# Head products in smaller pieces, value sums on TensorE for half of the heads stage, and half of the routing scatters behind the next root

## The chip, the core and the metric

The kernel runs on one core of a Trainium2 chip. The core has five engines that work side by side, each through its own queue in order: TensorE (PE in the profile, with PEld for its weight loads), VectorE (DVE), ScalarE (ACT), GpSimd (POOL) and SyncE (SP), which issues transfers here. The metric is the device time of one execution in microseconds (us), the median of several runs. Lower is better.

## The reference

The program is a decoder of two layers, all in fp32, on x of 4 sequences with 256 tokens of 256 features. Every step is `x = x + block(layernorm(x))`. Layer 0 has an attention with a compressed key and value, a cross attention over a context, and a block that routes one token in eight through attention and MLP. Layer 1 has three blocks, and two of them are what this case is about.

The first is an attention over the 16 heads *of one token*, with no product between tokens:

```python
qkv = x @ w_qkv.T + b_qkv                      # (b, n, 3, H=16, d=16)
attn = einsum('bnhd,bngd->bnhg', q, k) / sqrt(c)
attn = softmax(attn, axis=-1)
out  = einsum('bnhg,bngd->bnhd', attn, v)
out  = out.transpose(0, 2, 1, 3).reshape(b, n, c) @ w_out.T + b_out
```

Per token that is a 16x16 table of weights, and each is a sum over 16 products. Then follows a causal cross attention over the context with 16 heads, and last a mixture of 28 experts (width 176): a softmax over 28 gate values, the best six of them made to sum to one, and `y += w * (silu(x @ wg) * (x @ wu)) @ wd` for these six.

## The kernel before

**Layout and order.** The tokens lie on the 128 partitions: each sequence is two tiles of 128 tokens. The program is written as Python generators, which are advanced in turn by `_side_by_side` (L60) with weights, so that instructions of two stages come to lie beside each other. A scheduler then settles the order in each engine's queue from the dependencies. `_stay_behind` (L78) adds a dependency that only fixes the order of two instructions on one queue; no semaphore comes of it. Buffers come from pools; a tile with `bufs=1` can be written again only when its last reader is done.

**Heads stage** (`_head_attention`, L1422). `half(g)` does sequences 0 and 1 (g = 0), then 2 and 3 (g = 1), each in four steps j of 128 rows. `project` (L1475) computes q, k and v on TensorE, which ACT copies into `qkv`. `products` (L1501) lets GpSimd multiply every q by every k: four instructions of 128x1024 in each step, into two tiles `qk` (L1518 for g = 0, L1526 for g = 1). `weights` (L1535) sums them: for g = 0 on TensorE by 16 products with the identity for each half c of the heads, into the PSUM tile `as` (L1545); for g = 1 by DVE reduces (L1562). Then come maximum, subtraction and the exponential on ACT. `combine` (L1569) sums the weights on DVE (L1571), takes the reciprocal (L1573), scales the weights (L1574), multiplies by v into `pv` (128x2048, L1580) and reduces it into `O` (L1587), for each half c. At the end `O` is turned by TensorE (L1604), projected, and added to x (L1619). `products(j+1)` is written ahead of `combine(j)`. g = 0 stands beside the routed block of layer 0 (`_routed_block`: mask L1176, rope steps L1243 on DVE and L1250, L1253 on GpSimd, mpr L1345, maT L1361, and the addition L1310), and the layer-0 cross attention (L596); g = 1 beside the first half of the cross attention.

**Cross attention** (`_cross_attention`, L1628). Eight units for each sequence b. A unit computes scores `xsc` on TensorE, their maximum `cnm` on DVE (L1711, L1712), the exponential `xpr` on ACT (L1717), turns it in TensorE (`x_tp`) and copies it from PSUM to `xpT`: three copies of four on DVE (L1733), one on ACT (L1731). Then `xav`, the projection `xpo`, the addition to x (L1773), and `then(b)`, which starts the routing of that sequence while the units of the next go on. `xqT` (L1821) is the query of a pair of sequences.

**Routing** (`_route`, L698). For sequence b: POOL fills parts of `R` (L704, L706); `layernorm` takes mean and variance on DVE (`ln_ve`, L167), the inverse root by a `pow` on GpSimd (`ln_rs`, L154; the "root" below), and writes R on DVE (L172). TensorE turns it (`g_tp`, L714), computes gate values `pl` (L721), DVE copies them (`lg`, L723) and finds the best six; TensorE ranks the tokens of each expert (`rank`, L761, L762); DVE gives the target `rows` (L770) and the weights (L780). Then twelve indirect transfers by GpSimd, two tiles by six experts, scatter the rows of R into `lists` in memory (L786).

**Experts.** `_Blocks` (L879) works on blocks of 128 rows of `lists`: load `xb` (L917), turn (`tpx`, L923), `pgu` (L933), silu and product (`eh`, L939), turn (L944), the weight of each row (`wjunk`, L953), `py` (L964), `ys` (L968), and an adding scatter into `acc` (L969). There are 62 blocks; the first nine are loaded from GpSimd's queue, the others from SP's. The gate and up weights (`wgu_e`) are loaded after the heads stage, the down weights (`wdn_e`, L678) after the cross attention, both by SP. The nine early loads, the routing of sequence 3 and the first blocks stand beside one another.

Of the kernel before, what the change touches and what calls it, by code (L numbers as in the profile page):

```python
# [10 lines left out]
F32 = mybir.dt.float32  # L11
# [3 lines left out]
ALU = mybir.AluOpType  # L15
# [4 lines left out]
P = 128  # L20
# [99 lines left out]
def kernel(ctx: ExitStack, tc: tile.TileContext, w: dict, out: bass.AP):  # L120
    nc = tc.nc
# [28 lines left out]
    nc.gpsimd.tensor_tensor(root, root, neghalf, ALU.pow)  # L150

    def rsqrt(src, n, tag):
        r = sm.tile([P, n], F32, tag=tag, name=tag)
        nc.gpsimd.tensor_tensor(r, src, neghalf[:, :n], ALU.pow)  # L154
        return r
# [349 lines left out]
    for _ in range(4):  # L505
# [17 lines left out]
        turned32=cst[:, K_TURN:], blank=blank, psum=psum, sm=sm, cst=cst, ident=ident, identb=identb, maskb=maskb, tri=tri, ones=ones,  # L523
        ones_row=ones_row, layernorm=layernorm, ln_stats=ln_stats, ln_apply=ln_apply, rsqrt=rsqrt, transposed=transposed, ctxT=ctxT, neghalf=neghalf,
    )
# [111 lines left out]
    nc.sync.dma_start(wgt, w["e_gate"].rearrange("(k p) n -> p k n", p=P))  # L637
    route = dict(env, rt=rt, rt1=rt1, wgt=wgt, seen=seen, lists=lists)
    xatt = ExitStack()
# [37 lines left out]
    for g in range(0, E, 7):  # L677
# [3 lines left out]
        )  # L681
    blocks = _Blocks(ctx, nc, tc, dict(route, wgu=wgu, wdn=wdn, acc=acc))
    early = blocks.early(*route["early"])
    last = _route(nc, tc, x, B - 1, route)
    for _ in range(2):
        next(last)
    next(early)
    for _ in last:
# [6 lines left out]
def _route(nc, tc, x, b, env):  # L695
# [9 lines left out]
    for i in range(2):  # L705
        nc.gpsimd.iota(  # L706
            R[:, i, C : C + 1].bitcast(I32), [[0, 1]], base=(2 * b + i) * P, channel_multiplier=1
        )
    env["layernorm"](x[2 * b : 2 * b + 2], [R[:, i, :C] for i in range(2)])
    yield  # L710
    tp = psum.tile([P, 2, 2, P], F32, tag="tp", name="g_tp")
# [57 lines left out]
    rows = rt.tile([P, 2, TOPK], I32, tag="rows", name="rows")  # L769
    nc.vector.tensor_scalar(rows, top[:, :, :TOPK], -1.0, None, ALU.add)  # L770

# [8 lines left out]
    nc.vector.tensor_tensor(R[:, :, C + 1 : C + 1 + E], ex, wide(zt), ALU.mult)  # L780

    for n in range(TOPK):
        if b < B - 1 and n:
            yield
        for i in range(2):
            put = nc.gpsimd.indirect_dma_start(  # L786
                out=lists,
                out_offset=bass.IndirectOffsetOnAxis(ap=rows[:, i, n : n + 1], axis=0),
                in_=R[:, i, :],
                in_offset=None,  # L790
            )
            tc.declare_no_dep(put.ins, group="lists", reason="all rows of all of these differ")
            tc.add_to_no_dep_group("lists", put.ins)

# [84 lines left out]
class _Blocks:  # L879
# [5 lines left out]
    def __init__(self, ctx, nc, tc, env):  # L885
        self.nc, self.psum, self.cst, self.ident = (nc, env["psum"], env["cst"], env["ident"])
        self.wgu, self.wdn, self.lists, self.acc = (env[n] for n in ("wgu", "wdn", "lists", "acc"))
        self.ek = ctx.enter_context(tc.tile_pool(name="ek", bufs=2))
        self.eb = ctx.enter_context(tc.tile_pool(name="eb", bufs=EARLY + 2))
        self.puts = 0  # L890

# [22 lines left out]

    def load(self, row, queue):
        xb = self.eb.tile([P, ROW], F32, tag="xb", name="xb")
        queue.dma_start(xb, self.lists[bass.ds(row, P), :])  # L917
        return xb
# [30 lines left out]
    def down(self, hT, e, xb, e_col, accs):  # L949
        nc = self.nc  # L950
        wsel = self.ek.tile([P, 1], F32, tag="wsel", name="wsel")
        junk = self.ek.tile([P, E], F32, tag="wjunk", name="wjunk")
        nc.vector.scalar_tensor_tensor(  # L953
            junk,
            self.cst[:, K_IOTA : K_IOTA + E],
            e_col,
            xb[:, C + 1 : C + 1 + E],
            ALU.is_equal,
            ALU.mult,
            accum_out=wsel,  # L960
        )
        py = self.psum.tile([P, C], F32, tag="o", name="py")
        for k in range(2):
            nc.tensor.matmul(  # L964
                py, hT[:, k, :], self.wdn[:, bass.ds(e * (2 * C) + k * C, C)], start=(k == 0), stop=(k == 1)
            )
        y = self.ek.tile([P, C], F32, tag="ys", name="ys", bufs=NACC + 2)
        nc.scalar.activation(y, py, AF.Copy, scale=wsel)  # L968
        nc.gpsimd.indirect_dma_start(  # L969
            out=accs[self.puts % len(accs)],  # L970
            out_offset=bass.IndirectOffsetOnAxis(ap=xb[:, C : C + 1].bitcast(I32), axis=0),
            in_=y,
            in_offset=None,
            compute_op=ALU.add,
        )
        self.puts += 1

    def early(self, words, rows, e_all):
        at = self.values(rows, mybir.EngineType.Pool, TRASH, 0, EARLY)
        xbs = [self.load(r, self.nc.gpsimd) for r in at]  # L980
        yield
# [439 lines left out]
def _head_attention(nc, tc, x, w, env):  # L1421
# [6 lines left out]
    H = D = 16  # L1428
    Q = S // H

    a1 = env["stack"].enter_context(tc.tile_pool(name="ha1", bufs=1))
# [21 lines left out]
    def half(g):  # L1453
# [46 lines left out]
        def products(j):  # L1500
# [4 lines left out]
            for c in range(2):  # L1505
# [5 lines left out]
                else:  # L1511
                    q3 = qkv[:, 0:C].rearrange("p (h d) -> p h d", d=D)
                    k3 = qkv[:, C : 2 * C].rearrange("p (g d) -> p g d", d=D)
                    pr = a2.tile([P, 8, H, D], F32, tag="qk", name="qk")
                for i in range(2):
                    if g == 0:
                        dd = slice(8 * i, 8 * i + 8)
                        nc.gpsimd.tensor_tensor(  # L1518
                            pr[:, dd],
                            q3[:, dd, hh].unsqueeze(3).to_broadcast([P, 8, 8, H]),  # L1520
                            k3[:, dd].unsqueeze(2).to_broadcast([P, 8, 8, H]),
                            ALU.mult,
                        )
                    else:
                        h0 = 8 * c + 4 * i
                        nc.gpsimd.tensor_tensor(  # L1526
                            pr[:, 4 * i : 4 * i + 4],
                            q3[:, h0 : h0 + 4].unsqueeze(2).to_broadcast([P, 4, H, D]),
                            k3.unsqueeze(1).to_broadcast([P, 4, H, D]),
                            ALU.mult,  # L1530
                        )
# [37 lines left out]
        def combine(j, qkv, s):  # L1569
            ss = sm.tile([P, H], F32, tag="ass", name="ass")  # L1570
            nc.vector.tensor_reduce(ss, s, AX.X, ALU.add)  # L1571
            rs = sm.tile([P, H], F32, tag="ars", name="ars")
            nc.vector.reciprocal(rs, ss)  # L1573
            nc.vector.tensor_tensor(s, s, rs.unsqueeze(2).to_broadcast([P, H, H]), ALU.mult)  # L1574
            yield
            v3 = qkv[:, 2 * C :].rearrange("p (d g) -> p d g", g=H)
            for c in range(2):
                hh = slice(8 * c, 8 * c + 8)
                pv = a2.tile([P, 8, D, H], F32, tag="pv", name="pv", bufs=1)
                nc.vector.tensor_tensor(  # L1580
# [46 lines left out]
def _cross_attention(nc, tc, x, w, env):  # L1627
# [93 lines left out]

    def turned(pr, sp):
        pTs = []
        for j in range(2):
# [4 lines left out]
            pT = c3.tile([P, 3 * P], F32, tag=f"xpT{sp}{j}", name=f"xpT{sp}{j}", bufs=2)  # L1729
            if sp and j:  # L1730
                nc.scalar.copy(pT, tp.rearrange("p n q -> p (n q)"))  # L1731
# [52 lines left out]
    def after(f, b, g, e, sp, pr, ss):  # L1784
# [3 lines left out]
        if sp == 0:  # L1788
            state["pTs"] = turned(pr, sp)
            return  # L1790

        pTs = [one for two in zip(state["pTs"], turned(pr, sp)) for one in two]

# [184 lines left out]
```

## Time and profile before

| what | value |
|---|---|
| median of three runs | 864.11 us (860.93 to 864.4) |
| the profiled execution | 864.99 us |
| its span, first to last instruction | 863.3 us |
| mean granted TensorE clock | 0.887 of full |
| busy, PE / PEld / DVE / ACT / POOL | 693.8 / 456.4 / 531.1 / 295.9 / 323.3 us |
| L1518 and L1526, products on GpSimd | 16 of 2372 ns and 16 of 2371 ns mean |
| L1580, pv on DVE | 16 of 2576 ns mean, 2271 shortest, 4074 longest |
| L1587, reduce on DVE | 16 of 2271 ns mean |
| L1574, scaling of weights on DVE | 8 of 843 ns mean |
| L1545, sums on TensorE (128 products, two records each) | 256 records, 35.7 us |
| L1733 and L1731, copies of xpT on DVE and on ACT | 548 and 482 ns mean |
| L786, scatters on GpSimd | 48, 46.7 us |

How to read it: the profile shows one execution, 1.7 us shorter in its span than in its own time. "Busy" is the time in which an engine executes. A record is "start, length, engine, line, operation, output <- inputs"; in brackets stands how long the engine had been idle ahead of it and which instruction or transfer released it. PEclk is the TensorE clock that was granted, as a share of full speed. The chain of waits is followed back from the last instruction to what released each one.

The heads stage with g = 0 lies at about 300 to 430 us, with g = 1 at 430 to 550, the second half of the cross attention with the routing of sequences 1 and 2 at 565 to 645, the routing of sequence 3 and the first blocks at 645 to 699, and the other blocks from there to 850.

### The profile page before, as it was taken

The page shows a single profiled execution, that of the slowest core. Times are in us where ns is not written, and L with a number is a line of the kernel's source. Part 1 is how long each engine was busy: PE and PEld are TensorE (multiplying, and loading weights), DVE is VectorE, ACT ScalarE, POOL GpSimd, SP SyncE. Part 2 cuts the span into 40 slices and gives each one's busy share as a digit, 9 for nine tenths or more (in the row PEclk, how much of TensorE's full clock was granted, in tenths as well). Part 3 has the DMA queues.
Part 4 walks back from the last instruction along what each step waited for, and adds up shares of the span by engine and source line. Part 5 has one row for each costly group of instructions (what it writes and reads, how often), then busy time and mean ns, then how long its engine had stood idle before and what let it go on. Part 6 is the DMA issues. An engine that isn't in the chain of part 4 may idle for free. (4 is left out here: it accounts for less than half of the span.)

```text
span 863.3 us, 12247 instructions
## 1 busy us (share of the span) xinstructions
PE 693.8 (80%) x3902; PEld 456.4 (53%) x3902; DVE 531.1 (62%) x1322; ACT 295.9 (34%) x974; POOL 323.3 (37%) x277
## 2 busy tenths in 40 slices
PE   8988998598988878869659556978573989889991
PEld 4546556355555566466325234556442667657770
DVE  4677666986563798985549997757352423363332
ACT  2255444342441401221045224355231334324440
POOL 3332212214220365520145430052352675556663
PEclk9999999789999789978789957998685899999995
DMA  8999999400405200231400000680138686776656
GB/s 296 307 332 325 325 327 326 179 1 0 175 27 204 84 2 1 80 116 49 153 13 1 0 1 1 223 329 29 55 102 189 171 149 107 143 190 103 111 69 167
DMA packets 84739, 117.93 MB, mean 137 GB/s; under 512 B 5822, under 2 KB 71871, under 8 KB 84162
## 3 DMA queue, kind: packets, MB, share of 16 engines
q1 hardware_dynamic: 71346, 99.00, 35.4%
q0 software_dynamic: 11664, 16.54, 11.1%
q10 hardware_dynamic: 1664, 1.57, 0.6%
q8 instruction: 35, 0.57, 0.3%
q14 instruction: 30, 0.25, 0.1%
HBM read 59.66 MB, written 55.33 MB: 133 GB/s over the span
## 5 line engine op out<-in xcount | busy, mean ns | idle before, releaser
L969 POOL DMA_INDIRECT acc<-ys,xb x62 | 98.2, 1583 | 60.8 <-ACT Tx L925 50.3
L933 PE MATMUL pgu<-wgu_e,Tx 128*128 x248 | 91.4, 492 | 4.3 <-ACT Tx L925 3.7
L416 POOL TENSOR_TENSOR pr<-pr,rs 128x512 f32<-128x512 f32 x32 | 42.4, 1325 | 131.5 <-DVE rs L414 73.8
L406 ACT ACTIVATE pr<-sc,nb 128x256 f32<-128x256 f32 x128 | 59.0, 475 | 49.4 <-DVE nb L401 49.3
L786 POOL DMA_INDIRECT lists<-R,rows x48 | 46.7, 973 | 67.7 <-DVE rows L770 29.6
L1717 ACT ACTIVATE xpr<-xsc,cnm 128x256 f32<-128x256 f32 (+1 forms) x128 | 52.2, 422 | 53.9 <-DVE cnm L1712 47.3
L964 PE MATMUL py<-wdn_e,Th 88*128 x248 | 64.3, 384 | 3.7 <-DVE Th L946 3.7
L964 PEld LDWEIGHTS py<-wdn_e,Th 88*128 88x128 f32 x248 | 46.8, 192 | 20.5 <-DVE Th L946 5.6
L933 PEld LDWEIGHTS pgu<-wgu_e,Tx 128*128 128x128 f32 x248 | 44.1, 198 | 21.2 <-issue 3.2
L1526 POOL TENSOR_TENSOR qk<-qkv 128x1024 f32<-128x1024 f32 x16 | 37.4, 2371 | 38.5 <-ACT qkv L1497 26.4
L939 DVE TENSOR_TENSOR eh<-pgu,sg 128x176 f32<-128x176 f32 x62 | 21.1, 340 | 49.8 <-ACT sg L937 49.8
L105 PE MATMUL av<-pT,ckt 128*64 128x256 f32 x256 | 39.4, 404 | 14.8 <-DVE pT L432 9.9
L1545 PE MATMUL as<-qk,cst 128*128 128x128 f32 x256 | 35.7, 305 | 10.4 <-POOL qk L1518 10.4
L968 ACT ACTIVATE ys<-py,wsel 128x256 f32<-128x256 f32 x62 | 29.4, 474 | 41.5 <-PE py L964 38.1
L937 ACT ACTIVATE sg<-pgu 128x176 f32<-128x176 f32 x62 | 19.7, 318 | 69.4 <-PE pgu L933 69.4
L1518 POOL TENSOR_TENSOR qk<-qkv 128x1024 f32<-128x1024 f32 x16 | 37.5, 2372 | 13.8 <-ACT qkv L1490 7.1
L397 DVE TENSOR_REDUCE nm<-sc 128x4 f32<-128x1024 f32 x32 | 38.9, 1217 | 5.5 <-PE sc L105 5.2
L953 DVE SCALAR_TENSOR_TENSOR wjunk<-cst,e_all,xb 128x28 f32<-128x28 f32 x62 | 15.4, 248 | 42.5 <-ACT ys L968 37.7
L1545 PEld LDWEIGHTS as<-qk,cst 128*128 128x128 f32 x256 | 34.3, 219 | 13.2 <-POOL qk L1518 11.5
L1580 DVE TENSOR_TENSOR pv<-s,qkv 128x2048 f32<-128x2048 f32 x16 | 41.2, 2576 | 0.1
L108 PE MATMUL tp<-cst,pr 128*128 128x128 f32 x256 | 38.5, 293 | 2.4 <-DVE pT L432 1.5
L105 PE MATMUL sc<-ckv,qk 64*128 64x256 f32 x256 | 39.5, 410 | 0.8 <-ACT qk L383 0.8
(374 smaller groups left out, 1556.5 us busy)
## 6 DMA issues: line engine op xcount, KB each, us to landing
lists<-blank SPq DMA_DIRECT2D x9, 3600.0 KB, 28.5
wgu_e<-in_e_gu_dram SPq DMA_DIRECT2D x4, 2464.0 KB, 16.1
xb<-lists SPq DMA_DIRECT2D x53, 144.0 KB, 2.6
acc<-blank SPq DMA_DIRECT2D x5, 1152.0 KB, 11.2
wdn_e<-in_e_dn_dram SPq DMA_DIRECT2D x4, 1232.0 KB
wq<-in_m_wq_dram SPq DMA_DIRECT2D x4, 1024.0 KB, 6.7
mwo<-in_m_wo_dram SPq DMA_DIRECT2D x2, 2048.0 KB, 8.2
part<-acc SPq DMA_DIRECT2D x16, 256.0 KB, 4.4
```

The costliest lines, as they stand in the source:

```text
L105: self._next(self.engine.matmul(*args, **kw))
L108: self._next(self.engine.transpose(*args, **kw))
L397: nc.vector.tensor_reduce(nm, sc, AX.X, ALU.max, negate=True)
L406: nc.scalar.activation(pr[:, e, qt, :], sc[:, e, qt, :], AF.Exp, bias=nb[:, e, qt : qt + 1], accum_out=ss[:, e, qt : qt + 1],)
L416: nc.gpsimd.tensor_tensor(pr[:, 1], pr[:, 1], rs[:, 1].unsqueeze(2).to_broadcast([P, 2, S]), ALU.mult)
L786: put = nc.gpsimd.indirect_dma_start(out=lists, out_offset=bass.IndirectOffsetOnAxis(ap=rows[:, i, n : n + 1], axis=0), in_=R[:, i, :], in ...
L933: nc.tensor.matmul(pg, xT[:, k, :], self.wgu[:, bass.ds(e * (4 * M) + k * 2 * M, 2 * M)], start=(k == 0), stop=(k == 1))
L964: nc.tensor.matmul(py, hT[:, k, :], self.wdn[:, bass.ds(e * (2 * C) + k * C, C)], start=(k == 0), stop=(k == 1))
L969: nc.gpsimd.indirect_dma_start(out=accs[self.puts % len(accs)], out_offset=bass.IndirectOffsetOnAxis(ap=xb[:, C : C + 1].bitcast(I32), axi ...
L1545: nc.tensor.matmul(ps[:, c, :P], ident, prs[c][:, n].rearrange("p h g -> p (h g)"), start=(n == 0), stop=(n == D - 1),)
L1580: nc.vector.tensor_tensor(pv, s[:, hh].unsqueeze(2).to_broadcast([P, 8, D, H]), v3.unsqueeze(1).to_broadcast([P, 8, D, H]), ALU.mult,)
L1717: nc.scalar.activation(pr[:, j, cols], sc[:, j, cols], AF.Exp, bias=nm[:, i, j : j + 1], accum_out=ss[:, i, h : h + 1])
```

## The change

1. **Pieces.** The products of q and k on GpSimd are issued as four instructions of 512 elements for each tile, not two of 1024 (both g).
2. **Value sums on TensorE**, for g = 1. The weights are not scaled by the reciprocal. `pv` has the layout (g, h, d), so that both inputs are read in steps of 16 elements (64 bytes) along one dimension; sixteen products with the identity for each half c sum it over g into the PSUM tile `ao`, and one DVE operation for each j multiplies by the reciprocal into `O`. `pv` gets two buffers (both g).
3. **Scatters.** For b = 0 and 1 the last six of the twelve scatters are put off (`puts`) and issued, in the queue's order, behind the root of sequence b + 1. The nine early loads are ordered behind the root of sequence 3, and the first `wjunk` behind `rows` of sequence 3.
4. **Copies.** For b = 0 and 1, three of four `xpT` copies go to ACT and one to DVE.

GpSimd's queue from the routing of sequence 0 on is then: six scatters of sequence 0, root of 1, six scatters of 0, memset and iota of R for 2, six scatters of 1, root of 2, six of 1, memset and iota of R for 3, twelve of 2, root of 3, nine loads, twelve of 3. Before it was: twelve of 0, memset and iota for 2, root of 1, twelve of 1, memset and iota for 3, root of 2, twelve of 2, two loads, root of 3, seven loads, twelve of 3. TensorE's order around sequence 3 stays. In the second half of the heads stage the sums `ao` stand between the cross units on TensorE, two of them ahead of each `pqkv` but the first two. In the first half, the last two `pv` now stand ahead of the routed block's second `mpr` and of both `maT`, where one stood ahead of that `mpr` and the other between the two `maT` before.

The core of the diff:

```diff
     def rsqrt(src, n, tag):
         r = sm.tile([P, n], F32, tag=tag, name=tag)
-        nc.gpsimd.tensor_tensor(r, src, neghalf[:, :n], ALU.pow)
+        roots.append(nc.gpsimd.tensor_tensor(r, src, neghalf[:, :n], ALU.pow))
         return r
...
     env["layernorm"](x[2 * b : 2 * b + 2], [R[:, i, :C] for i in range(2)])
+
+    root = env["roots"][-1]
+    for put in env["puts"]:
+        _stay_behind(tc, put(), root)
+    env["puts"] = []
+    env["root"] = root
     yield
...
     for n in range(TOPK):
         if b < B - 1 and n:
             yield
         for i in range(2):
...
+            if b < B - 2 and n >= TOPK // 2:
+                env["puts"].append(functools.partial(put, n, i))
+            else:
+                put(n, i)
...
-    def load(self, row, queue):
+    def load(self, row, queue, behind=None):
         xb = self.eb.tile([P, ROW], F32, tag="xb", name="xb")
-        queue.dma_start(xb, self.lists[bass.ds(row, P), :])
+        done = queue.dma_start(xb, self.lists[bass.ds(row, P), :])
+        if behind is not None:
+            _stay_behind(self.tc, done, behind)
         return xb
...
+        if not self.puts:
+            _stay_behind(self.tc, done, self.route["placed"])
...
-                for i in range(2):
+
+                for i in range(4):
                     if g == 0:
-                        dd = slice(8 * i, 8 * i + 8)
+                        dd = slice(4 * i, 4 * i + 4)
...
                     else:
-                        h0 = 8 * c + 4 * i
+                        h0 = 8 * c + 2 * i
...
+            if g == 1:
+
+                v3 = qkv[:, 2 * C :].rearrange("p (d g) -> p g d", g=H)
+                ps = psum.tile([P, 2, 8, D], F32, tag="o", name="ao")
+                for c in range(2):
+                    hh = slice(8 * c, 8 * c + 8)
+                    pv = a2.tile([P, H, 8, D], F32, tag="pv", name="pv", bufs=PV)
+                    nc.vector.tensor_tensor(
+                        pv,
+                        s[:, hh].rearrange("p h g -> p g h").unsqueeze(3).to_broadcast([P, H, 8, D]),
+                        v3.unsqueeze(2).to_broadcast([P, H, 8, D]),
+                        ALU.mult,
+                    )
+                    yield
+                    for n in range(H):
+                        nc.tensor.matmul(
+                            ps[:, c].rearrange("p h d -> p (h d)"),
+                            ident,
+                            pv[:, n].rearrange("p h d -> p (h d)"),
+                            start=(n == 0),
+                            stop=(n == H - 1),
+                        )
+                    yield
+                nc.vector.tensor_tensor(
+                    O[:, :, j, :],
+                    ps.rearrange("p c h d -> p (c h) d"),
+                    rs.unsqueeze(2).to_broadcast([P, H, D]),
+                    ALU.mult,
+                )
+                return
             nc.vector.tensor_tensor(s, s, rs.unsqueeze(2).to_broadcast([P, H, H]), ALU.mult)
...
-                pv = a2.tile([P, 8, D, H], F32, tag="pv", name="pv", bufs=1)
+                pv = a2.tile([P, 8, D, H], F32, tag="pv", name="pv", bufs=PV)
...
-            if sp and j:
+
+            if (sp and j) if b >= 2 else (sp or j):
                 nc.scalar.copy(pT, tp.rearrange("p n q -> p (n q)"))
```

## The prediction

> **What bounds the kernel now.** I read the windows by stage first, then the chain of waits, then the timelines of the engines at its waits. The windows (core time, then busy time and instructions of PE, PEld, DVE, ACT, POOL, the granted clock, DMA) part the stages:
>
> ```profile
> 320.00:430.00 110.00, 86.37 (x501) 60.32 (x500) 82.05 (x125) 19.19 (x55) 36.96 (x29) 0.86 0.22 73
> 430.00:550.00 120.00, 81.79 (x501) 47.46 (x499) 96.75 (x122) 44.99 (x163) 39.15 (x18) 0.82 0.04 11
> 565.00:660.00 95.00, 63.82 (x484) 45.24 (x482) 48.18 (x163) 33.08 (x140) 42.12 (x53) 0.79 0.39 124
> ```
>
> From 430 to 550 (heads of sequences 2 and 3 beside cross attention) DVE leads with 97 of 120 us, and in finer windows it is busy 20.00 of the 20 us from 480. From 565 to 660 (cross attention and routing) no engine is two thirds busy: waits set the time. The chain of waits there runs through GpSimd's scatters:
>
> ```profile
> 609.51 2.43 DMA lists<-R,rows
> 612.04 2.45 DMA lists<-R,rows
> 614.90 0.70 POOL ln_rs L154
> 616.18 0.66 PE g_tp L714 x2
> ...
> 643.38 9.32 DMA lists<-R,rows
> ```
>
> and TensorE's timeline shows what they cost (start, length, instruction, in brackets the idle time before it and its releaser):
>
> ```profile
> 584.06 0.66 PE L714 MATMUL g_tp<-cst,R 128*128 128x128 f32 x2 [5.58 <-DVE R L172]
> ...
> 616.18 0.66 PE L714 MATMUL g_tp<-cst,R 128*128 128x128 f32 x2 [8.48 <-DVE R L172]
> ...
> 656.01 1.09 PE L714 MATMUL g_tp<-cst,R 128*128 128x128 f32 x4 [12.89 <-DVE R L172]
> ...
> 663.34 0.69 PE L923 MATMUL tpx<-cst,xb 128*128 128x128 f32 x2 [3.13 <-DVE lg L723]
> ```
>
> R waits for the root on GpSimd, and the root for its queue. After 699 the expert blocks follow one another, paced by TensorE (pgu and py), to the end: I take that tail to shift rigidly.
>
> **Scatters behind the root.** The root of sequence 1 could run when ln_ve exists; GpSimd was elsewhere:
>
> ```profile
> 576.44 0.41 DVE L167 TENSOR_SCALAR ln_ve<-ln_mv 128x2 f32<-128x2 f32 x1
> ```
> ```profile
> 579.72 0.96 POOL L786 DMA_INDIRECT lists<-R,rows  x1 [0.30 <-issue]
> 582.51 0.11 POOL L704 MEMSET R<- 128x6 f32 x1 [1.83 <-issue]
> ...
> 582.75 0.72 POOL L154 TENSOR_TENSOR ln_rs<-ln_ve,neghalf 128x2 f32<-128x2 f32 x1
> ```
>
> A scatter takes 0.96 + 0.30 between two = 1.27 us; twelve occupy GpSimd from 565.52 to 580.68. With six deferred it is free at 573.1, before ln_ve at 576.9. Root 0.72, R 0.41 and a hand-over of 0.15 to 0.5 put g_tp at about 578.4, where TensorE arrives at 578.5: 5.58 becomes 0.3, gain **5.3**. For sequence 2, ln_ve is there at 607.9 and six scatters from 598.02 end at 605.6. Root, R and hand-over give 609.3 against TensorE free at 607.7: 8.48 becomes 1.6, gain **6.9**.
>
> The deferred six, 7.6 us, and the memset, which waits 1.6 to 1.8 for the last of them to be read, now lie behind the root. For sequence 1 this ends at 577.7 + 7.6 + 2 = 587; the next rows come at 592.5 (598.0 less 5.3), so they fit with 5 us left. For sequence 2 it ends near 612.5 on the shortened clock against rows near 614: 1.5 us left. If that is eaten, the last scatters land later, and the early loads with them: I take **+0.5**, from 0 to +2. Nobody reads the deferred rows before those loads.
>
> At sequence 3 the root leaves the loads (654.67, behind two of them) for 645.2, ahead of nine. That does not start the experts: the first tpx needs xb, which needs the 9.32 us landing of the last scatter (beside the wdn_e weights, issued from 643.15) and 8.8 of its own load. The loads start where they did. What goes is lg waiting on DVE behind wjunk: xb landed at 662.07 and tpx began at 663.34, so **1.2**. The rank at 668.82 stays behind pgu on TensorE.
>
> After each gap TensorE is slow: the same sixteen xav take 1.51 us at 585.84 and 0.86 at 594.09; six x_tp 1.54 against 0.87; eight xsc 1.36 against 0.92. One gap costs 1.8 us in these rows. The Trainium skill (TensorE: Matmul & The Clock Gate, "Why this matters for your kernels") says that idle gaps over about 3 us drop the clock. By that rule, both gaps being under 3 afterwards, both penalties go in full, 1.8 and about 3. The granted clock rows are less kind: 0.73 in 620 to 640 with TensorE busy 18.45 of 20 us. I take **3**, between 0 and 5.
>
> Sum: −5.3 − 6.9 − 1.2 − 3 + 0.5 = **−15.9**, from −9 to −19.
>
> **Sums on TensorE, and copies to ACT (second half).** DVE loses 8 reduces of L1587 at 2.27 (18.2 us), four L1574 (0.42 clean, up to 2.44: say 4), and 16 copies at 0.55 (8.8). It gains four O operations reading PSUM, 0.42 each as L1619. Net −29 us of 97. ACT gains 16 x 0.48 = 7.7 on 45 of 120: hidden. The eight pv now read s and v in 64-byte steps, as no DVE row here does. Below: 2.28, the clean pv row; above: twice that, +18 on DVE. VectorE: DVE Perf Modes ("Mode 1× (REGULAR) — the baseline") holds that plain fp32 makes no assumption on strides; I take 2.28.
>
> TensorE gains 128 products of fp32 128x128. The row for the same shape is
>
> ```profile
> L1545 PE MATMUL as<-qk,cst 128*128 128x128 f32 x256 | 35.7, 305 | 10.4 <-POOL qk L1518 10.4
> ```
>
> with two records to a product; on the timeline 32 to 36 records pass in 4.2 us, so 0.25 us a product, 32 us in all (36 by busy time). Here the skill speaks for a far better deal: the clock page's "Back-to-back issue gap" gives about 81 ns for N = 128, hence 10 us. The row decides, since it has this type and shape; by the rule TensorE would stay far from full, by the row it fills up: 81.8 + 32 = 114 of 120 us, less what a warmer clock returns (0.82 now). So the bound passes from DVE to TensorE. One sum of 16 products (4.2 us) also stands where a 2.27 us reduce stood in the chain pv, O. And pqkv of the next step stands behind two such sums on TensorE, 8.4 us, with the qk of GpSimd waiting for it; the xsc units stand behind them too, and their cnm on DVE. Against that, DVE waits such as 7.61 us of TensorE on xpT at 499.26 vanish. Walking the new order by these durations, O of the last step comes at 522 to 525 instead of 530.5, but about two cross units are left over that were done before; xqT of the second half, which ends the stage, comes at 556 to 560 instead of 560. I take **−2**, from +6 to −8.
>
> **Products in pieces of 512 (both halves).** 32 instructions become 64. A clean piece should take about half of 2.03 plus a start: L416, also 512 wide, has a mean of 1.325, clean L1250 1.27, so 1.05 to 1.3, or 0.1 to 0.5 for each of 32 extra, 3 to 9 us of GpSimd, which idles two thirds of these stages; on the path only where qk is waited for, some 2 us. What it buys: DVE operations with two SBUF inputs stand while a product runs:
>
> ```profile
> 479.79 4.07 DVE L1580 TENSOR_TENSOR pv<-s,qkv 128x2048 f32<-128x2048 f32 x1
> ```
>
> Clean, this pv is 2.28; the excess of 1.8 is nearly one whole product. I sum such excesses to 17 us on DVE in the first half (L1580, L1574, L1176, L1243, L596, L1310). If a stall lasts to the end of the running piece, half, 8 us, goes; about 5 of it lies on the routed chain. Against it: two pv buffers let the scheduler put both last pv ahead of the routed block's mpr and maT, up to two more operations of 2.28, about +1.8 there once other waits overlap, and GpSimd's extra +1 in the rope steps (L1250, L1253). Net **−2**, from +3 to −6.
>
> **Total.** −15.9 − 2 − 2 = −19.9 on the profiled execution's 864.99 (span 863.3 and 1.7 around it): **845**. The median of the runs is 0.9 lower, within my rounding.
>
> **Rivals.**
> 1. *The routing waits are replaced.* For: only 1.5 us of cover at sequence 2, and the landing beside wdn_e (9.32 against 2.45) may grow. Then the first wait's 5.3 and 1.2 are kept, 6.9 and the clock are halved, +2 is paid: −9.5; heads nothing: **855**.
> 2. *The heads give all their room.* DVE's full stretch was the bound and TensorE's clock warms to 1.00, as in 460 to 480 with 17.97 busy: −8 and −5 beside −17: **835**.
> 3. *TensorE as the new bound; slower.* Place: 449 to 550. At the slow clock of that stage (0.15 a record) the 128 products cost 38 us, as much as all idle there (120 − 81.8 = 38.2), and idle cannot be packed: each of eight sums then adds its 4.2 in full, 34 us, less the 8 of shortening I granted and the 16 of routing: +10, **875**. It decides from the point where the heads stage loses more than 20 us, that is when over 60% of the new products fall outside the idle time. Against it: DVE's own work drops by 29 us, so TensorE's waits on DVE shrink.
> 4. *Order eats all.* The stage loses 12 to 18 (or pv pays its +18 for the strides), cancelling routing: **863**.
>
> **Numbers.** A measurement of this kernel tells about 0.5%, 4.3 us, from no change. Forecast 0.51 (838 to 852), rival 1 0.18, rival 2 0.11, rival 4 0.09, rival 3 0.11. Faster: 0.51 + 0.18 + 0.11 = 0.80; same 0.09; slower 0.11. The range 829 to 863 leaves out rival 3 and a little at each end.
>
> **What would show it.** Right: g_tp waits under 2 us at sequences 1 and 2, the root of sequence 3 before the first load, tpx still waiting for xb; ao at about 4.2 us for a sum, TensorE above 90% from 449 to 540; pv near 2.28 with excesses under 1.2; the block tail as long as before. Wrong: pv near 4.5 in the second half; xqT of the second half later than 565; a memset or scatter on GpSimd that waits longer than 2 us ahead of the root; lists landing later than 9.3 after its last scatter.

## The result, and the profile after

The changed kernel takes 876.12 us (875.0 to 877.25, four runs) against 864.01 for the kernel before (four runs beside it): a ratio of 1.0148, 95% interval 1.0121 to 1.0175. It is slower; 845 had been forecast. Its profiled execution took 875.67 us, its span is 873.7, or 10.4 more than before. Code below the first part of the change has other line numbers now (pv of the second half is L1603, the sums are L1611, the scatters L792, the root L157).

The first view is the windows again, cut this time at events that both kernels have: from the first products of the second half of the heads to the last `o_tp`, from there to the last `xqT`, and on to the issue of the wdn_e loads, which follows the end of the cross attention. Of before:

```profile
437.90:535.40 97.50, 59.56 (x381) 34.61 (x380) 84.93 (x90) 37.59 (x135) 37.45 (x16) 0.79 0.00 1
535.40:560.90 25.50, 23.89 (x156) 15.17 (x154) 18.80 (x65) 10.05 (x41) 1.71 (x2) 1.00 0.50 186
560.90:643.20 82.30, 64.71 (x514) 45.58 (x514) 48.18 (x162) 35.49 (x149) 36.04 (x43) 0.83 0.34 127
```

The same three of the changed kernel:

```profile
442.50:553.20 110.70, 85.00 (x623) 64.23 (x621) 67.45 (x68) 37.94 (x133) 40.49 (x32) 0.85 0.00 1
553.20:585.30 32.10, 28.65 (x175) 18.82 (x171) 19.03 (x70) 14.84 (x57) 4.88 (x6) 0.89 0.75 281
585.30:653.20 67.90, 62.26 (x510) 43.81 (x510) 46.57 (x154) 36.26 (x151) 33.58 (x41) 0.90 0.25 93
```

The routing stretch fell by 14.3 us, near the sum that was worked out. The two stretches of the heads grew by 13.2 and 6.6: TensorE (the first busy number) gained 25 us, VectorE (the third) lost 17, and the stage became longer though VectorE is now idle for two fifths of it. The first half of the heads (first products to the products of the second half) went from 139.5 to 144.6. So −0.6 ahead of it, +5.2 + 19.8 − 14.3, and +0.3 behind: 10.4.

TensorE's waits in the routing, the answer to the four lines shown of before:

```profile
603.65 0.44 PE L723 MATMUL g_tp<-cst,R 128*128 128x128 f32 x2 [0.47 <-DVE R L175]
...
626.24 0.41 PE L723 MATMUL g_tp<-cst,R 128*128 128x128 f32 x2 [1.60 <-DVE R L175]
...
656.49 0.67 PE L723 MATMUL g_tp<-cst,R 128*128 128x128 f32 x4 [3.27 <-DVE R L175]
...
668.17 0.66 PE L941 MATMUL tpx<-cst,xb 128*128 128x128 f32 x2 [8.41 <-DMA xb<-lists]
```

0.47 and 1.60 us stand where 5.58 and 8.48 stood. The wait of sequence 3 went from R to xb, as expected, and the end does not hang on it: the first `py` waits for the down weights.

```profile
693.02 3.75 PE L984 MATMUL py<-wdn_e,Th 88*128 x8 [3.37 <-DMA wdn_e<-in_e_dn_dram]
```

They were issued at 653.24, 10.1 us later than before, and the end came 10.4 later: from that issue to the end it is 220.5 us against 220.2.

In the second half of the heads, VectorE's waits (instruction, releaser, us in all, times, longest). Before:

```profile
DVE s L1562 <- POOL qk L1526: 11.9, 4, 7.9
```

After:

```profile
DVE s L1584 <- POOL qk L1548: 28.4, 8, 8.2
```

VectorE waits 16.5 us more for the next products than before. The wait near the end of the stage has changed too. Before, TensorE waited for VectorE's O of the last step:

```profile
526.02 0.44 PE L1604 MATMUL o_tp<-cst,O 128*64 128x128 f32 x1 [7.00 <-DVE O L1587]
```

After, VectorE waits for TensorE's last sums, and these had waited for pv:

```profile
534.42 6.03 PE L1611 MATMUL ao<-pv,cst 128*128 128x128 f32 x32 [5.11 <-DVE pv L1603]
```
```profile
544.71 0.42 DVE L1619 TENSOR_TENSOR O<-ao,ars 128x256 f32<-128x256 f32 x1 [5.50 <-PE ao L1611]
```

GpSimd's timeline says why the products are waited for; each line is one step's products, of before and then of after:

```profile
437.93 9.21 POOL L1526 TENSOR_TENSOR qk<-qkv 128x1024 f32<-128x1024 f32 x4 [10.68 <-ACT qkv L1497]
461.56 9.23 POOL L1526 TENSOR_TENSOR qk<-qkv 128x1024 f32<-128x1024 f32 x4 [14.41 <-ACT qkv L1497]
472.11 9.61 POOL L1526 TENSOR_TENSOR qk<-qkv 128x1024 f32<-128x1024 f32 x4 [1.33 <-ACT qkv L1497]
493.84 9.40 POOL L1526 TENSOR_TENSOR qk<-qkv 128x1024 f32<-128x1024 f32 x4 [12.13 <-DVE s L1562]
```
```profile
442.51 9.77 POOL L1548 TENSOR_TENSOR qk<-qkv 128x512 f32<-128x512 f32 x8 [10.12 <-ACT qkv L1518]
467.68 9.80 POOL L1548 TENSOR_TENSOR qk<-qkv 128x512 f32<-128x512 f32 x8 [15.40 <-ACT qkv L1518]
490.78 10.71 POOL L1548 TENSOR_TENSOR qk<-qkv 128x512 f32<-128x512 f32 x8 [13.30 <-ACT qkv L1518]
513.57 10.20 POOL L1548 TENSOR_TENSOR qk<-qkv 128x512 f32<-128x512 f32 x8 [12.07 <-ACT qkv L1518]
```

Before, the products of step 2 followed those of step 1 by 10.5 us; after, by 23.1, since qkv came late. Before, `pqkv` of that step began 5.9 us behind the products of step 1:

```profile
467.45 0.32 PE L1481 MATMUL pqkv<-b1rows,onesb 3*128 3x384 bf16 x1
```

After, it began 14.9 us behind them. TensorE's order there is two sums `ao` with units beside them, and then `pqkv`:

```profile
468.46 3.74 PE L1611 MATMUL ao<-pv,cst 128*128 128x128 f32 x32
...
473.21 3.74 PE L1611 MATMUL ao<-pv,cst 128*128 128x128 f32 x32
...
478.39 0.39 PE L106 MATMUL xsc<-masks,identb 128*128 128x256 bf16 x2
482.62 0.47 PE L1502 MATMUL pqkv<-b1rows,onesb 3*128 3x384 bf16 x1 [3.83 <-ACT xpr L1769]
483.02 2.93 PE L1504 MATMUL pqkv<-w1qkv,hT 128*128 128x384 f32 x4
```

### The profile page after: what moved, and what is told of

Same layout as the page of the kernel before. It is cut to its first block, busy times and chain, and to the rows that moved or that the text cites. A ratio compares the mean times of both kernels' runs of the same rounds, so it can differ in the third digit from the quotient of the medians.

```text
span 873.7 us, 12787 instructions
## 1 busy us (share of the span) xinstructions
PE 721.4 (83%) x4158; PEld 486.4 (56%) x4158; DVE 508.0 (58%) x1298; ACT 301.6 (35%) x990; POOL 330.7 (38%) x309
## 5 line engine op out<-in xcount | busy, mean ns | idle before, releaser
L989 POOL DMA_INDIRECT acc<-ys,xb x62 | 97.5, 1573 | 67.0 <-ACT Tx L943 55.7
L419 POOL TENSOR_TENSOR pr<-pr,rs 128x512 f32<-128x512 f32 x32 | 42.4, 1326 | 131.3 <-DVE rs L417 68.9
L984 PE MATMUL py<-wdn_e,Th 88*128 x248 | 67.8, 401 | 6.7 <-DMA wdn_e<-in_e_dn_dram 3.4
L984 PEld LDWEIGHTS py<-wdn_e,Th 88*128 88x128 f32 x248 | 49.0, 201 | 24.0 <-issue 4.7
L792 POOL DMA_INDIRECT lists<-R,rows x48 | 46.9, 978 | 38.9 <-DVE rows L779 13.2
L1548 POOL TENSOR_TENSOR qk<-qkv 128x512 f32<-128x512 f32 x32 | 40.5, 1307 | 50.9 <-ACT qkv L1518 50.9
L1540 POOL TENSOR_TENSOR qk<-qkv 128x512 f32<-128x512 f32 x32 | 42.9, 1375 | 11.2 <-issue 11.2
L1567 PEld LDWEIGHTS as<-qk,cst 128*128 128x128 f32 x256 | 33.9, 213 | 10.5 <-POOL qk L1540 9.4
L109 PEld LDWEIGHTS tp<-cst,pr 128*128 128x128 f32 x256 | 30.5, 150 | 15.5 <-issue 13.4
## 6 DMA issues: line engine op xcount, KB each, us to landing
xb<-lists SPq DMA_DIRECT2D x53, 144.0 KB, 2.6
```

The source lines that it names most:

```text
L109: self._next(self.engine.transpose(*args, **kw))
L419: nc.gpsimd.tensor_tensor(pr[:, 1], pr[:, 1], rs[:, 1].unsqueeze(2).to_broadcast([P, 2, S]), ALU.mult)
L792: done = nc.gpsimd.indirect_dma_start(out=lists, out_offset=bass.IndirectOffsetOnAxis(ap=rows[:, i, n : n + 1], axis=0), in_=R[:, i, :], i ...
L984: nc.tensor.matmul(py, hT[:, k, :], self.wdn[:, bass.ds(e * (2 * C) + k * C, C)], start=(k == 0), stop=(k == 1))
L989: nc.gpsimd.indirect_dma_start(out=accs[self.puts % len(accs)], out_offset=bass.IndirectOffsetOnAxis(ap=xb[:, C : C + 1].bitcast(I32), axi ...
L1540: nc.gpsimd.tensor_tensor(pr[:, dd], q3[:, dd, hh].unsqueeze(3).to_broadcast([P, 4, 8, H]), k3[:, dd].unsqueeze(2).to_broadcast([P, 4, 8, H]),
```

## The experiments

**Theory A**: the routing change works; the heads lost the time through the strided `pv` and through the place of `pqkv` behind the sums. Rivals: **B**, the routing waits are only replaced; **C**, the pieces on GpSimd cost both halves; **D**, TensorE's added work itself is on the path. The runs were made in four groups, each on one chip with the kernel before beside it; a ratio is to that. The kernel before took 879 us on the chip of groups e and f, 864 on that of g, 867 on that of h: compare ratios across groups, and microseconds within one. The stretches (cut as above; "first half" from the first products to those of the second half) are of the profiled executions:

| run | ratio (95%) | first half | second half to o_tp | o_tp to xqT | xqT to wdn_e |
|---|---|---|---|---|---|
| before | 1 | 139.5 | 97.5 | 25.5 | 82.3 |
| after | 1.0148 (1.0121 to 1.0175) | 144.6 | 110.7 | 32.1 | 67.9 |
| e1 scatters | 0.9936 (0.9912 to 0.9961) | 139.7 | 97.5 | 25.5 | 89.8 |
| e2 pieces | 1.0015 (0.9998 to 1.0032) | 143.0 | 98.2 | 25.5 | 98.4 |
| e3 sums | 1.0243 (1.0186 to 1.0299) | 143.6 | 110.5 | 31.9 | 97.0 |
| e4 no sums | 0.9984 (0.9962 to 1.0006) | 144.1 | 101.0 | 28.0 | 88.5 |
| f1 after again | 1.0164 (1.0116 to 1.0213) | 144.8 | 110.7 | 32.1 | 88.6 |
| f2 v turned | 1.0088 (1.0059 to 1.0116) | 144.2 | 106.7 | 32.3 | 83.9 |
| f3 half sums | 1.0079 (1.0048 to 1.0111) | 144.7 | 102.1 | 33.1 | 86.0 |
| f4 late sums | 1.0107 (1.0067 to 1.0147) | 144.6 | 107.4 | 32.1 | 86.7 |
| g1 first half as before | 1.0096 (1.0063 to 1.0128) | 139.8 | 111.1 | 32.1 | 68.0 |
| g2 one product | 1.0008 (0.9980 to 1.0037) | 144.4 | 98.4 | 33.2 | 67.6 |
| g3 paced | 1.0118 (1.0052 to 1.0184) | 144.2 | 114.5 | 28.1 | 67.8 |
| g4 mended | 0.9950 (0.9929 to 0.9970) | 139.9 | 103.5 | 26.4 | 67.9 |
| h1 scatters, copies | 0.9774 (0.9735 to 0.9814) | 140.7 | 95.4 | 28.0 | 64.9 |
| h2 mended, old copies | 0.9899 (0.9861 to 0.9937) | 139.6 | 103.7 | 25.5 | 67.5 |
| h3 scatters, two pv | 0.9891 (0.9853 to 0.9930) | 144.0 | 100.5 | 25.4 | 67.8 |
| h4 scatters again | 0.9820 (0.9774 to 0.9867) | 140.1 | 97.5 | 25.5 | 67.9 |

**e1, the scatters alone.** The edit is the third part of the change on the kernel before.

> The kernel before, with the scatters alone put off (and the loads and the first wjunk ordered as in the change). Theory A (the routing change works, the heads stage lost the time): from xqT of the second half to the end of the cross attention 14 us go, so about 850 us. Theory B (the waits are only replaced by others on a chain that was not bound by them): within 3 us of before, about 862.

0.9936: neither number, on a chip whose routing stretch is longer for every kernel (last section). Within that group it gained 7 to 9 us in the stretch (89.8 against 98.4 and 97.0). On the chip of group h the same kernel (h4) gave what A said: 67.9 and 0.982. B falls. h4 has the scatters without the copies, so the 14 us are the scatters' own (its median is 15 us below that of before on its chip).

**e2, the pieces alone.**

```diff
-                for i in range(2):
+                for i in range(4):
```

> The kernel before, with the products of GpSimd in pieces of 512 alone (one pv buffer as before). Theory A: 4 to 5 us slower, about 868, if the first half's loss comes from the pieces themselves; about 862 or less if it comes from the second pv buffer and its order. Theory C (the pieces cost both heads stages, and the sums on TensorE little): 10 us slower or more, about 875.

The profiled execution shows 3.5 us lost in the first half and 0.7 in the second; the total does not differ from before within its interval, on a chip where the routing stretch alone varies by more. C falls: the second half hardly notices the pieces. What VectorE's timeline shows in the first half is another order. Before:

```profile
372.73 2.38 DVE L1580 TENSOR_TENSOR pv<-s,qkv 128x2048 f32<-128x2048 f32 x1
...
377.16 0.69 DVE L1337 TENSOR_REDUCE mnm<-msc 128x4 f32<-128x512 f32 x1 [2.05 <-PE msc L1329]
```

In e2:

```profile
367.67 2.29 DVE L1588 TENSOR_REDUCE O<-pv 128x128 f32<-128x2048 f32 x1
378.76 0.69 DVE L1337 TENSOR_REDUCE mnm<-msc 128x4 f32<-128x512 f32 x1 [8.80 <-PE msc L1329]
379.37 2.28 DVE L1581 TENSOR_TENSOR pv<-s,qkv 128x2048 f32<-128x2048 f32 x1
```

The second `pv` is queued behind the routed block's `mnm` now, which waits 8.80 us for TensorE; before, it stood ahead. Later the second `mpr` starts at 392.07, where it was 387.63. The pieces did shorten the stalls (the mask L1176 among them: 5.9 us in all before, 3.7 in the changed kernel). That the new order gave it back is read from these timelines; no run changed the order alone.

**e3, the sums alone, and e4, all but the sums.** e3 is the second part of the change on the kernel before; e4 is the changed kernel with

```diff
-            if g == 1:
+            if g == 2:
```

> The kernel before, with the value sums on TensorE for the second half alone (two pv buffers, copies of xpT and products as before). Theory A: the strided pv (3.6 us for 2.28) and the place of pqkv behind the sums cost the heads stage 15 to 20 us, so about 880. Theory C: within 5 us of before.

> The changed kernel with the value sums of the second half back on VectorE (pieces, two pv buffers, scatters and copies as in the change). Theory A: xqT of the second half comes some 15 to 20 us earlier than in the change, and the time is about 856 to 860. Theory C: within 5 us of the changed kernel, about 874.

e3 costs 19.4 us in the second half (142.4 against 123.0) and 21 in the total, near the 15 to 20 of A; e4 takes 13.7 off the changed kernel there, a little less than A said. The sums with what belongs to them are the cause of most of the loss in that half. e4 stays 6 us above before in that half, which A had not foreseen.

**f1 to f4, what in the sums.** f1 is the changed kernel again. f2 turns v while it is copied out of PSUM:

```diff
-            for i in range(2):
-                nc.scalar.copy(qkv[:, i * 384 : (i + 1) * 384], pq[:, i, :384])
+            nc.scalar.copy(qkv[:, :384], pq[:, 0, :384])
+            nc.scalar.copy(qkv[:, 384 : 2 * C], pq[:, 1, :P])
+            nc.scalar.copy(
+                qkv[:, 2 * C :].rearrange("p (g d) -> p d g", d=D), pq[:, 1, P : P + C].rearrange("p (d g) -> p d g", g=H)
+            )
...
-                v3 = qkv[:, 2 * C :].rearrange("p (d g) -> p g d", g=H)
+                v3 = qkv[:, 2 * C :].rearrange("p (g d) -> p g d", d=D)
```

f3 sums `range(0, H, 2)` in place of `range(H)`, which leaves out every second product. f4 keeps both pv of a step and issues their sums after the products of the next but one step:

```diff
         for j in range(4):
             after = (yield from products(j + 1)) if j < 3 else None
-            yield from combine(j, *now)
+            yield from late
+            late = (yield from combine(j, *now)) or ()
...
+        yield from late
```

Left out here is the move of the sums into a function, which `combine` returns.

> The changed kernel once more, so that the next three stand beside it on one chip. Both theories: 1 to 1.5% slower than before.

> The changed kernel, with v turned by the copy out of PSUM (ACT, one more instruction a step), so that pv reads v contiguously. Theory A (strided pv and the place of pqkv cost the heads stage): pv falls from 3.6 to about 2.3 us if the stride of v is what makes it slow, and 6 to 10 us go. Theory D (TensorE's 32 us of added work is the bound): pv may fall, the time within 3 us of the changed kernel.

> The changed kernel with only every second of the sixteen products in each value sum: half of the sum over g is left out. Takes 16 us of work from TensorE. Theory A: 2 to 5 us go (the sums are short waits in front of pqkv and of the last O). Theory D: 10 us or more go.

> The changed kernel with the sums of step j issued behind pqkv of step j+2: the same work in another order. Theory A: products of step 2 start some 8 to 12 us earlier against step 1 than in the change, and 6 to 10 us go. Theory D: within 3 us of the changed kernel.

Of the second half's 142.8 us, f2 takes 3.8, f3 7.5 and f4 3.2. The medians fell by more, 8.2, 8.9 and 5.8 us; but in the profiled executions the routing stretch, which these edits leave alone and which varies on that chip (last section), is shorter too, by 4.7, 2.6 and 1.9, so the stage's own length is taken. The stride of v is what made pv slow; this is the tile's row (shortest, median, longest in ns) of the changed kernel and of f2:

```profile
L1603 DVE TENSOR_TENSOR pv<-s,qkv x8: 3508/3619/3643, 456.7 to 535.6; 128x2048 f32<-128x2048 f32 x8
```
```profile
L1606 DVE TENSOR_TENSOR pv<-s,qkv x8: 2225/2254/2282, 456.5 to 531.3; 128x2048 f32<-128x2048 f32 x8
```

1.36 us less, eight times, is 10.9 us on VectorE, of which 3.8 reached the end of the stage. f4 did what it should to the products of step 2 (10.8 us behind step 1, not 23.1), yet gave 3.2. Each gave less than the 6 to 10 us that A expected, so neither cause alone carries the loss, and A falls as it was stated. f3 lies between its numbers and those of D, 7.5 us for 16 us of TensorE's work. D had called TensorE's added work the bound. TensorE is not full (it is busy 77% of the stretch), but its added work stands in the round of waits that sets the stage.

**g1 to g3.** g1 gives the first half its products of 1024 and a pv buffer of its own (tag `pv0`, one buffer); g2 sums `range(1)`, which leaves out fifteen products of sixteen; g3 restores one step in the emission:

```diff
             if g == 1:
-
+                yield
                 v3 = qkv[:, 2 * C :].rearrange("p (d g) -> p g d", g=H)
```

> The changed kernel with the first half of the heads as before: products of 1024, one pv buffer for it. Theory A (order on VectorE and GpSimd in the last step of the first half lost the time): the stretch from the first products to those of the second half goes from 144.7 back to about 139.5 us, and 4 to 5 us of the total go. Rival: the stall of pv behind whole products comes back and eats it: within 1.5 us of the changed kernel.

> The changed kernel with one product of each sixteen: fifteen sixteenths of every value sum are left out. VectorE keeps its relief, TensorE gets almost none of the new work. Theory D (TensorE's added work is the largest term): the second half's stretch, 142.8 us in the change, goes on falling in line with the half sums (135.2), to about 128 us; it stays above the 123 of before, since the strides of pv remain. If VectorE's relief were worth what its 29 us suggest, it would fall below 120.

> The changed kernel with one more step a round in the emission of the heads, as before the change, so that as many cross units stand beside the heads as before. If the units left over are what lost the 6.6 us between the last o_tp and xqT: about 5 us go in total. If the stage is bound by its sum of work: within 2 us of the changed kernel, the gain behind o_tp lost ahead of it.

g1: 139.8, as expected; the first half's loss goes with its two edits, and the rival (stalls that come back) falls. g2: with fifteen sixteenths of TensorE's sums gone, the second half takes 131.6, or 11.2 less. Its first stretch:

```profile
445.30:543.60 98.30, 60.80 (x383) 35.96 (x381) 68.89 (x68) 38.42 (x133) 51.54 (x32) 0.77 0.00 1
```

TensorE has 60.8 us of work there, as before (59.6), VectorE 68.9 where it had 84.9, and the stretch lasts 98.3 against 97.5, with a unit fewer done in it. The waits (of TensorE, then of VectorE) show what took the place of VectorE's work:

```profile
PE ao L1611 <- DVE pv L1603: 15.1, 6, 6.7
```
```profile
DVE s L1584 <- POOL qk L1548: 20.2, 6, 8.2
```

The products of step 2 start 17.0 us behind those of step 1 in g2, where it was 10.5 before: `pqkv` still stands behind units and waits 4.1 us for the exponential of one. TensorE waits for pv mostly in the last two steps. So 16 us less of VectorE's work brought nothing in this order. It does not follow that VectorE cost no time before: its timeline of before has no wait from 472 to 531 us, and TensorE waited for its O at the end of the stage.

g3 brings the units back in (28.1 behind o_tp, not 32.1) and pays for them ahead of it (114.5, not 110.7): the second half is as long as before that edit. That was the second case of its expectation.

**g4, all mends together.** v turned, late sums, the step restored, first half and products as before, with the scatters and copies of the change.

> Scatters and copies of the change, and value sums on TensorE with all that the other runs say: v turned, sums behind pqkv, the step of emission restored, products of 1024 and the first half as before. Theory A with D: the heads' second half costs still 6 to 8 us more than before (the 32 us of TensorE), the scatters give 5 to 6: within 0.4% of before. If the mends are worth all of the loss: like the scatters alone, 0.994 of before or less.

129.9 in the second half, 6.9 more than before: the first case's 6 to 8 us. The ratio, 0.9950, lies a little below its 0.4%, since the scatters gave 14 us on this chip, not 5 to 6. The mends are worth 13 us in that half. By the single runs they come to 3.8 (f2), 3.2 (f4), 0.2 (g3) and 0.7 (e2), or 7.9, so the effects do not simply add.

**h1 to h4, copies and the second buffer.** h1 is the third and fourth part of the change, h2 is g4 with `if sp and j:` as before, h3 is e1 with `bufs=2` for pv, h4 is e1.

> The kernel before with the scatters and with the copies of xpT moved to ACT, nothing else. If the copies cost the 5 us (ACT's exponentials stand behind copies that wait for TensorE): second half's stretch near 128 us, total near before. If they cost nothing: 123 us, total like the scatters alone.

> The mended sums (v turned, sums behind pqkv, the step restored, first half as before, products of 1024, scatters) with the xpT copies as before. If the copies cost the 5 us: second half's stretch falls from 129.9 to about 125 us and 4 to 5 us go. If the sums themselves hold it: it stays at 129 to 130, or rises since VectorE gets 9 us of copies back.

> The kernel before with the scatters and a second pv buffer, nothing else. First half's stretch 143.6 us as in the sums alone (139.7 without): 4 us lost there by the order of pv and mpr. If the second buffer also costs the 5 us of the second half: 128 there; otherwise 123.

> The scatters alone, on the chip of the three above. Routing stretch 68 us where the chip has no further stops in it, 14 us less than before; 0.985 to 0.994 of before.

The copies cost nothing (h1: 123.4), so it is not they that hold the mended version (h2, without them: 129.2). The second buffer costs 4 us in the first half and 2.9 in the second (h3: 125.9), half of what was in question. h1 beats both kernels: 847.67 us, 0.9774 of before. Whether the copies gain anything on top of the scatters is not shown: h1 takes 847.67 us and h4 852.74, but their intervals overlap between 0.9774 and 0.9814, only 3.0 of the 7.3 us between their profiled executions lie in the routing stretch, and g4 and h2, with the copies and without, have the same stretch (67.9 and 67.5). The routing stretch of h1 is the shortest of all:

```profile
561.80:626.70 64.90, 59.21 (x510) 41.84 (x510) 46.36 (x154) 36.17 (x151) 33.41 (x41) 0.95 0.40 148
```

TensorE is busy 59 of 65 us at 0.95 of its clock; in the kernel before it was 65 of 82 at 0.83.

## Why the prediction was wrong

- **Scatters, −15.9: right in mechanism and nearly in size.** −14.3 in the stretch. The two waits became 0.47 and 1.60 where 0.3 and 1.6 were worked out. h4, which has the scatters alone, shows the same 67.9 us. The clock rose from 0.83 to 0.90 and TensorE's busy time fell by 2.4, near the 3 taken between rule and row. The 1.2 at sequence 3 was not to be had: the first `py` waits for the down weights, and the time from their issue to the end did not change. The chain that I read at xb was not the last one.
- **Sums on TensorE, −2: wrong, +19.8.** The step that failed is the walk of the new order. It put 128 products, 32 us, into TensorE's idle time while VectorE was relieved by 29 us, and had the last O at 522 to 525 us, 5.5 to 8.5 earlier than before. The last O came at 545.1: 102.6 us behind the first products of this half, where it had been 92.6. The count and the price of the products were right (34.3 us busy, a sum 3.7 us at full clock). The idle was not free. It is where TensorE waits in a round that goes products, reduce, exponential, pv, qkv of a later step, with the units' scores, maxima and exponentials queued in between on three engines, and work put into TensorE's part of the round lengthens the round (f3: 7.5 us come back with half of the products, g2: 11.2 with fifteen sixteenths). The working names the wait itself, `pqkv` and the products behind two sums, but no loss from it is left in the result; VectorE's wait for the products grew by 16.5 us. Before, VectorE was in the way at the end of the stage. With its relief these waits took its place, and in g2 the relief bought nothing.
- **Rival 3.** It named this place, with each sum added in full, at 34 us, and got a tenth of the chance. That its 875 lies 1 us from the measured time is luck in part: the sums do not add in full (in g2 11.2 us came back for some 30 left out), and the stride, the second buffer and the first half made up for it.
- **The terms inside it.** pv in 64-byte steps was taken at 2.28 us, the lower end; it measured 3.6, between the ends. The Trainium skill's sentence on the baseline mode of VectorE (VectorE: DVE Perf Modes, "Mode 1× (REGULAR) — the baseline") was read as a statement of speed and is one of what works; f2 shows the stride to cost 1.36 us a pv, 3.8 us of the stage. The 81 ns for N = 128 of the Trainium skill (TensorE: Matmul & The Clock Gate, "Back-to-back issue gap") were rightly set behind the row: sixteen fp32 products, 32 records, passed in 3.74 us at full clock, 234 ns a product. The second buffer cost 2.9 (h3), the pieces 0.7 (e2); with the 11.2 of g2 and the 3.8 of f2 that is 18.6, near the 19.8. Since the effects do not simply add (g4), this is no proof of the shares. The 3.2 of the place of pqkv (f4) probably lie within the 11.2; no run had both edits. The two units left over were seen, and g3 shows that they are not a loss of their own.
- **Pieces, −2: wrong, +5.2.** Shorter stalls came (the six groups named took 6.6 us less of VectorE in the first half, near the 8 that were worked out; two others, `spread` and `ln_ve`, took 1.7 more), but the stage did not end sooner. The order of the last step had been priced at +1.8. In h3, with two buffers, the second `mpr` starts 8.7 us behind the first; in e1, with one, it was 4.3. In e1, then in h3:

```profile
381.49 0.68 DVE L1365 TENSOR_TENSOR mpr<-mpr,mrs 128x512 f32<-128x512 f32 x1
...
383.56 2.29 DVE L1600 TENSOR_TENSOR pv<-s,qkv 128x2048 f32<-128x2048 f32 x1
385.77 0.69 DVE L1365 TENSOR_TENSOR mpr<-mpr,mrs 128x512 f32<-128x512 f32 x1
```
```profile
384.31 0.68 DVE L1365 TENSOR_TENSOR mpr<-mpr,mrs 128x512 f32<-128x512 f32 x1
...
386.38 4.49 DVE L1600 TENSOR_TENSOR pv<-s,qkv 128x2048 f32<-128x2048 f32 x2
390.79 2.28 DVE L1607 TENSOR_REDUCE O<-pv 128x128 f32<-128x2048 f32 x1
392.99 0.68 DVE L1365 TENSOR_TENSOR mpr<-mpr,mrs 128x512 f32<-128x512 f32 x1
```

  Two pv and a reduce, 6.8 us, lie between the two `mpr` in place of one pv; the routed block waits for the second. In the changed kernel it is 8.4 us. Each of the two edits alone loses 3.5 to 4.3 us in this half, with an order of its own (e2, h3), and both together 5.2; taking both away gives 4.9 back (g1).

What stays open: how the 19.8 us divide between TensorE's work, its place and the stride; the pieces were not tried with VectorE's order of before held fixed, so what shorter stalls alone are worth in the first half isn't known; and of the 6 us that the mended sums still cost, 2.9 may be the second buffer, which they need.

## What to carry to other kernels

Ahead of moving work from a full engine to an idle one, ask whether the idle time lies in the same round of waits as the work that would leave: then it is not room, and the stage can lengthen although every engine's total would fit. Relief of the engine that bounds a stage is worth only what the next round of waits leaves over; a run that gives the relief and leaves the new work out (here one product of sixteen) tells it at once. A queue in order makes every edit an edit of order: look at what stands behind a moved or newly waiting instruction, and price it by the whole group that passes, not by one operation.

## What the runs showed of the hardware

A VectorE product of two SBUF operands, 128x2048 in fp32, takes 3.6 us when one of them has an innermost step of 64 bytes (changed kernel, f1) and 2.25 when it is read in one piece (f2). The step of 64 bytes in s, which is not the innermost one, stayed in f2 and costs nothing: pv of before, without it, took 2.27 at the shortest.

On the chip of groups e and f all eight profiled executions had stops in the routing stretch that the ten on the other chips did not show. In e2 PE, ACT and VectorE stood together for 2 to 5 us while scatters ran, with no transfer of data named as the releaser:

```profile
648.25 0.48 ACT L1732 COPY xpT<-x_tp 128x384 f32<-128x384 f32 x1 [5.40 <-remote]
...
648.78 0.21 PE L835 MATMUL pn<-cst,seen 128*28 128x1 f32 x1 [3.99 <-issue]
...
649.63 0.15 DVE L837 COPY cnt<-pn 28x1 f32<-28x1 f32 x1 [2.29 <-issue]
```

e2 and e3, whose routing is that of before, take 97 to 98 us there, against 82 for before on the first chip. In e2 the stops of over 1 us that name no other engine and no transfer come to 9.4 us on TensorE, where before has none, and TensorE's busy time is 8.6 us longer (73.4 against 64.7, at a clock of 0.77 against 0.83). The two together are about the difference. What causes the stops was not tried.
